# Separate rooms for results in a two-bottleneck kernel: five rooms for chunks, four for results, five for weights

## The chip, the cores and the metric

The kernel runs on one core of a Trainium2 chip, in one launch. The metric is the device time of the whole program in microseconds (us); before the change it is 2444.54 us, the median of three runs (2437.88 to 2444.91). The profiled execution, from which all other times here come, has a span of 2434.0 us.

## What is computed

The input is x with 16 images of 1024 channels and 32 x 32 pixels in float32. Two residual bottlenecks follow one another. Cut to what matters:

```python
# layer 0
h = relu(bn(conv1x1(x, w_conv1)))                 # 1024 -> 256 channels
q, k, v = relu(bn(h*wq)), relu(bn(h*wk)), bn(h*wv)  # 1x1 convolutions, 256 -> 256
att = softmax over the 3x3 neighbourhood of q . (k + pos), 32 heads of 8 channels
h = relu(bn(sum of v over the neighbourhood, weighted by att))
y = relu(bn(conv1x1(h, w_conv3)) + x)             # 256 -> 1024, residual x
# layer 1
g = relu(bn(conv1x1(y, w1)))                      # 1024 -> 256
g = relu(bn(conv3x3(g, w2)))                      # 256 -> 256
out = relu(bn(conv1x1(g, w3)) + y)                # 256 -> 1024, residual y
```

## The kernel before

An image's 1024 channels are eight chunks of 128 channels by 1024 pixels, 512 KB each. The work of the 16 images is cut into stages, whose order is written out by hand (L934 to L938): C (first 1x1 convolution, eight chunks of x), Q and V (projections to q, k and v), F (fused: third convolution of layer 0, residual x, and at once the first convolution of layer 1), W (the 3 x 3 convolution in Winograd form, four images at a time), U (last 1x1 convolution, residual y, output). Stages of different images follow each other on TensorE; a planner (`Side`, from L837) puts the attention's VectorE work and the Winograd transforms between them by estimated times. The program order on each engine is the order in which the Python code emits instructions; an engine's queue is worked off strictly in that order.

One chunk of an F or U stage goes through class `Expand` (from L367). `seed` (L375) has ScalarE (ACT) copy the residual chunk from SBUF into a PSUM tile, two chunks ahead of use. `products` (L381) lets TensorE add the eight matmul passes of the 1x1 convolution to it. `result` (L396) has ACT add the shift and apply relu, from PSUM into SBUF, and GpSimd (POOL) issues the store. In F the store goes to a DRAM room (`r`), and the SBUF result is also read by the eight passes of the next convolution (`reduce_part`, L348). In U the store goes to the output. The residual of an F stage is called s (read from x), that of a U stage r (read back from the DRAM room).

Before the change the result is written over the residual: `self.tiles[o]` keeps the tile that the seed has read, and `result` takes it again. So one of the eight rooms of the pool `xpool` serves a chunk from the start of its load to the landing of its store. The same eight rooms hold the chunks of x for the C stages and the V tiles (transformed hidden rows) of the W stages.

`more_loads` (L312) issues loads in the order of a fixed list, so long as there are credits; almost all go through POOL's queue, where the stores of results and the relays of the attention (q, k, v and position tables, L535) stand too. `free` (L334) gives a credit back. After a result it is called with `late`, which holds one credit back until the next call. The credits only set the place of a load in the queue: at run time the load waits until the room it was given is free, that is until the last reader, or the store, of its former tile is done.

Weights come in pieces of 512 KB through the SP queue (`more_weights`, L111) into `wpool`, six rooms. Four pieces are asked for at the start, and each piece done with asks for the next, so at most four are wanted at a time; pieces of w3 and u1 are loaded anew for every F stage, pieces of the others are kept if they are used again within three stages. A W stage reads 18 pieces U, each for one group of 16 matmul passes.

PSUM holds four tiles of 128 x 1024. Waits between engines and for rooms are put in by the framework.

Of the kernel before, what the change touches and what calls it, by code (L numbers as in the profile page):

```python
# [8 lines left out]
F32 = mybir.dt.float32  # L9
AF = mybir.ActivationFunctionType  # L10
# [3 lines left out]
P = 128  # L14
B, C, H, W = 16, 1024, 32, 32
HW = H * W
# [6 lines left out]
HEAD_DIM = 8  # L23
EPS = 1e-5
RELU = AF.Relu
CHUNKS = 8
NJ = 4
JROWS = H // NJ
JPIX = JROWS * W
# [7 lines left out]
NK = 4  # L37
# [9 lines left out]
PART = LINES * TR  # L47
# [24 lines left out]
def sa_bottleneck_kernel(ctx: ExitStack, tc: tile.TileContext, x, w1t, wqkvt, w3t, u1t, u2t, u3t, params, out):  # L72
    nc = tc.nc
# [1 line left out]
    ctx.enter_context(tc.manual_schedule())  # L75

    const = ctx.enter_context(tc.tile_pool(name="const", bufs=1))
    wpool = ctx.enter_context(tc.tile_pool(name="wpool", bufs=6))
    xpool = ctx.enter_context(tc.tile_pool(name="xpool", bufs=CHUNKS))
    hpool = ctx.enter_context(tc.tile_pool(name="hpool", bufs=5))  # L80
    apool = ctx.enter_context(tc.tile_pool(name="apool", bufs=1))
    ppool = ctx.enter_context(tc.tile_pool(name="ppool", bufs=2))
# [224 lines left out]
        return slice(half * HALF, (half + 1) * HALF)  # L307


    loads, loaded, stored, credits, freed = [], {}, {}, [CHUNKS], []  # L310

    def more_loads():  # L312

        while credits[0] and loads:
            kind, b, c = loads[0]
            if kind == "V":

                if forms.get((b, c[1] == 2), 0) < NK:
                    return
                src = form_room(b)[c[0], c[1]].rearrange("p k j e -> p (k j e)")  # L320
            elif kind == "r":
                if (b, c) not in stored:
                    return
                src = stored[b, c]
            else:
                src = x[b, c * P : (c + 1) * P, :]
            t = xpool.tile([P, NK * 2 * PART], F32, tag="x", name=f"{kind}_{b}_{c}".translate(str.maketrans(" ,", "__", "()")))
            t = t if kind == "V" else t[:, :HW]

            (nc.scalar if kind == "x" and b == 0 else nc.gpsimd).dma_start(t, src)  # L330
            loaded[loads.pop(0)] = t
            credits[0] -= 1

    def free(late):  # L334

        if late:
            freed.append(1)
            credits[0] += len(freed) - 1
            del freed[1:]
        else:  # L340
            credits[0] += 1 + len(freed)
            freed.clear()
        more_loads()

    def piece(name, half):
# [21 lines left out]
    class Expand:  # L367
# [2 lines left out]

        def __init__(self, name, b, kind, shift):
            self.name, self.b, self.kind, self.shift = name, b, kind, shift
            self.ahead, self.tiles = {}, {}

        def seed(self, o):  # L375
            ps = psum.tile([P, HW], F32, tag="ps", name="ps")
            t = self.tiles[o] = loaded.pop((self.kind, self.b, o))
            nc.scalar.activation(ps, t, AF.Identity)  # L378
            self.ahead[o] = ps

        def products(self, o):  # L381
            key = piece(self.name, o * 2 // NC)
# [11 lines left out]
                done_with(key)  # L394

        def result(self, o, to):  # L396
            t = self.tiles.pop(o)
            ps, to_ = self.ahead.pop(o), t

            if self.kind == "s":  # L400
                ps, to_ = ps.rearrange("p (n j) -> p j n", j=4), t.rearrange("p (j n) -> p j n", j=4)
            else:
                ps, to_ = ps.rearrange("p (j n) -> p n j", j=4), t.rearrange("p (n j) -> p n j", j=4)
            if (self.kind, self.b, o) == ("r", B - 1, NC - 1):

                one, two = slice(0, JPIX // 2), slice(JPIX // 2, JPIX)
                nc.scalar.activation(to_[:, one], ps[:, one], RELU, bias=self.shift(o), scale=1.0)
                nc.vector.tensor_scalar(to_[:, two], ps[:, two], self.shift(o), 0.0, ALU.add, ALU.max)
                nc.scalar.dma_start(to[:, :HALF], t[:, :HALF])
                nc.sync.dma_start(to[:, HALF:], t[:, HALF:])  # L410
                return t
            nc.scalar.activation(to_, ps, RELU, bias=self.shift(o), scale=1.0)  # L412
            nc.gpsimd.dma_start(to, t)  # L413
            return t
# [301 lines left out]
    def winograd_conv(b):  # L716
# [12 lines left out]
        def products(i, two):  # L729

            if i not in acc:
                acc[i] = psum.tile([P, 2, NK, NW, TILES], F32, tag="ps", name="ps")
            key = piece(f"U{i}", two)
            v = loaded.pop(("V", b, (i, two))).rearrange("p (k j e) -> p j k e", k=NK, j=2)
            for at in range(2):

                start = two == 0 or (two == 2 and at == 1)
                for n in range(NW):
                    for m in range(NW):
                        nc.tensor.matmul(  # L740
                            acc[i][:, at, :, n, :],
                            pieces[key][:, m, at, n * P : (n + 1) * P],
                            v[:, at, :, m * (TILES + TR) :][:, :, :TILES],
                            start=(start and m == 0 and n == 0),
                            stop=(m == NW - 1),
                            skip_group_check=True,
                        )
            done_with(key)
            free(False)

        def pair(t):
            return t.rearrange("p (a n t) -> p a n t", a=2, t=TILES)
# [181 lines left out]
    for text in (  # L934
# [5 lines left out]
        for word in text.split():  # L940
            b, _, of = word[1:].partition(":")
# [41 lines left out]
    def first_conv(b):  # L983

        ps = two_sums()
        for c in range(NC):
            reduce_part(c, ps, loaded.pop(("x", b, c)), "w1")
            free(False)
            if c == NC - 1:
                h = hidden[b] = hpool.tile([P, NW, HW], F32, tag="h", name=f"h_{b}")  # L990
                for n in range(NW):
                    nc.scalar.activation(  # L992
                        h[:, n, :], ps[n], RELU, bias=col("L0_conv_bn1_b", n), scale=col("L0_conv_bn1_s", n)
                    )
            yield CHUNK
# [22 lines left out]
    def fused(b, then):  # L1018

        side.finish(b)  # L1020
        if b == B - 1:
            for c in DEFERRED:
                side.first(transform(c, sources[c]) if c in sources else fetched(c), 0.0, 0.0)
        fetch_attended()
        side.until(side.ready[b])
        finish_attended(b)
        conv3 = expand("w3", b)
        conv3.src = attended.pop(b)
        following = [(conv3, o) for o in range(2, NC)] + then
        done, ps = {}, None  # L1030
        for o in range(NC + 1):
            if o < NC:
                conv3.products(o)
                room = stored[b, o] = dram.tile([P, HW], F32, tag=f"r{b}_{o}", name="r")
                done[o] = conv3.result(o, room)
                if o < len(following):
                    into, which = following[o]
                    into.seed(which)
                yield CHUNK
            if o:  # L1040
                ps = ps or two_sums()
                reduce_part(o - 1, ps, done.pop(o - 1), "u1")
                free(True)
                if o == NC:
                    side.finish_firsts()
                    for n in range(NW):
                        nc.scalar.activation(
                            hidden_rows(n), ps[n].rearrange("p (j r c) -> p j r c", j=4, c=TR), RELU,
                            bias=bn_sh[:, n : n + 1], scale=bn_inv[:, n : n + 1],
                        )  # L1050
                    if b in DEFERRED:
                        kept[b] = dram.tile([P, NW * VROWS * VW], F32, tag=f"h{b}", name="kept")
                        nc.sync.dma_start(kept[b], vh.rearrange("p r w -> p (r w)"))
                    else:
                        late = 0.0 if b % NK == NK - 1 else LATE
                        side.first(transform(b, vh), side.tensor + CHUNK + 6.0, side.tensor + late)
                yield CHUNK

    def last_sum(b, of, then):

        last = expand("u3", b)
        last.src = hidden_one[b]
        following = [(last, o) for o in of[2:]] + then
        for at, o in enumerate(of):
            last.products(o)
            if at < len(following):
                into, which = following[at]
                into.seed(which)
            last.result(o, out[b, o * P : (o + 1) * P, :])
            free(True)  # L1070
            yield CHUNK

    def seeds(at):
# [9 lines left out]
    def run(at):  # L1083
        now[0] = at
        kind, b, of = stages[at]
# [20 lines left out]
        for part in range(count):  # L1106
            if alone and then and part >= count - 2 and kind != "wino":
                into, which = then[part - count + 2]

                if which not in into.ahead and which not in into.tiles:  # L1110
                    into.seed(which)
            if made and (kind, part) in (("conv1", 4), ("u3", count - 2)):
                finish_winograd(made.pop(0))
# [76 lines left out]
```

## Time and profile before

| | |
|---|---|
| median of three runs | 2444.54 us |
| span of the profiled execution | 2434.0 us |
| TensorE matmuls (PE) busy | 2388.0 us, 98% |
| VectorE (DVE) busy | 2080.7 us, 85% |
| ScalarE (ACT) busy | 918.9 us, 38% |
| GpSimd (POOL) busy | 466.2 us, 19% |
| moved by DMA | 708.37 MB, mean 291 GB/s |
| store of a result to the output, issue to landing | 6.5 us (median) |
| load of a residual r | 5.7 us |
| load of a residual s | 6.2 us |
| load of a Winograd weight piece U | 6.8 us |

A group in the profile reads: line, engine, operation, what it writes and reads, shapes and count; then busy time and mean of one; then the time that the engine stood idle just before such instructions, and what released it. Timeline lines read: start and length in us, engine, line, operation, count, and in brackets the idle time before it and its releaser. Matmuls are pipelined and their ends are modelled, so start-to-start times say more than busy time. A float32 matmul of the program appears as two passes.

### The profile page before, as it was taken

Reading aid. Unit: us, or ns where it says so; the run is one execution under the profiler, and the core shown is the slowest. Engines: PE = TensorE matmul, PEld = TensorE weight load, DVE = VectorE, ACT = ScalarE, POOL = GpSimd, SP = SyncE. Lnnn points to the kernel's source line nnn. Section 1 sums busy time; section 2 is a strip of 40 time slices with the busy share of each in tenths; the row PEclk is TensorE's granted clock in tenths of the full one; section 3 lists DMA queues with packets and bytes.
Section 4 is the critical chain, followed back from the end, with each engine's and each line's share of the span. In section 5 each row is a group of like instructions: output and inputs, shape, how many; then the busy total and the mean of one; then the engine's idle time right before and its main releaser. Section 6 shows DMA issues by size and latency. Waiting matters only on the chain.

```text
span 2434.0 us, 18415 instructions
## 1 busy us (share of the span) xinstructions
PE 2388.0 (98%) x6144; PEld 1150.9 (47%) x6144; DVE 2080.7 (85%) x1632; ACT 918.9 (38%) x873; POOL 466.2 (19%) x854
## 2 busy tenths in 40 slices
PE   8999999999999989999999999999999999999999
PEld 3434444444475434444466434444466444444843
DVE  4899999999999999898989999799989999965700
ACT  3324142323122564443122564324222453344265
POOL 2211111111121222111111222111111221111122
PEclk9999999999999999999999999999999999999999
DMA  9968786878697899798788899688788896888888
GB/s 364 368 211 283 278 253 246 281 273 258 246 370 262 296 306 347 252 315 262 256 312 280 288 306 358 242 305 301 263 314 296 286 351 249 290 311 299 329 258 277
DMA packets 305821, 708.37 MB, mean 291 GB/s; under 512 B 20544, under 2 KB 174144, under 8 KB 297024
## 3 DMA queue, kind: packets, MB, share of 16 engines
q0 software_dynamic: 119024, 471.40, 55.0%
q1 hardware_dynamic: 185264, 231.30, 29.1%
q10 hardware_dynamic: 1440, 4.51, 0.5%
q8 instruction: 49, 0.80, 0.1%
q14 instruction: 44, 0.36, 0.0%
HBM read 432.10 MB, written 275.03 MB: 291 GB/s over the span
## 4 chain that ended last, share of the span: by engine, by line
PE 72%; DMA 11%; issue 5%; DVE 3%; POOL 2%; ACT 1%; SPq 0%; POOLq 0%; ACTq 0%; DVEq 0%
PE ps L354 32%; PE ps L385 21%; PE ps L448 11%; PE ps L740 7%; DMA out_dram<-r 7%; DMA bnk<-kp 1%; DMA U<-uw 1%; POOL r L330 1%; PE ps L486 1%; DVE acc L605 1%; DMA s<-in_x_dram 1%; DVE acc L618 1%; ACT h L992 0%; DMA pos<-by_offset 0%; POOL out_dram L413 0%
## 5 line engine op out<-in xcount | busy, mean ns | idle before, releaser
L385 PE MATMUL ps<-a,w 128*128 128x512 f32 x1024 | 460.3, 594 | 4.9 <-ACT a L644 3.0
L385 PE MATMUL ps<-y,u 128*128 128x512 f32 x1024 | 447.4, 598 | 13.8 <-ACT ps L378 13.8
L354 PE MATMUL ps<-s,u 128*128 128x512 f32 x1024 | 458.0, 592 | 2.2 <-ACT s L412 2.2
L354 PE MATMUL ps<-x,w 128*128 128x512 f32 x1024 | 443.6, 594 | 6.3 <-DMA x<-in_x_dram 6.3
L605 DVE TENSOR_TENSOR acc<-e,bnv 128x2048 f32<-128x2048 f32 x144 | 327.5, 2284 | 3.6
L554 DVE TENSOR_TENSOR prod<-qc,bnk 128x2048 f32<-128x2048 f32 x144 | 324.0, 2287 | 1.7
L385 PEld LDWEIGHTS ps<-y,u 128*128 128x128 f32 x1024 | 195.9, 192 | 263.4 <-issue 241.2
L412 ACT ACTIVATE s<-ps,par 128x1024 f32<-128x1024 f32 x128 | 142.6, 1114 | 469.0 <-PE ps L385 401.2
L385 PEld LDWEIGHTS ps<-a,w 128*128 128x128 f32 x1024 | 194.7, 191 | 252.4 <-issue 242.7
L354 PEld LDWEIGHTS ps<-x,w 128*128 128x128 f32 x1024 | 195.1, 191 | 251.5 <-issue 250.3
L354 PEld LDWEIGHTS ps<-s,u 128*128 128x128 f32 x1024 | 194.4, 190 | 247.6 <-issue 238.2
L618 DVE TENSOR_TENSOR acc<-acc 128x2048 f32<-128x2048 f32 x128 | 293.4, 2292 | 4.4
L448 PE MATMUL ps<-h,wqk 128*128 128x512 f32 x512 | 227.8, 599 | 10.5 <-ACT h L992 10.5
L413 POOL DMA_DIRECT2D r<-s x128 | 68.8, 538 | 632.7 <-ACT s L412 608.4
L412 ACT ACTIVATE r<-ps,bn_sh 128x1024 f32<-128x1024 f32 x127 | 140.5, 1107 | 83.9 <-PE ps L385 83.1
L559 DVE TENSOR_TENSOR prod<-prod 128x2048 f32<-128x2048 f32 (+1 forms) x80 | 166.2, 2077 | 2.4
L448 PEld LDWEIGHTS ps<-h,wqk 128*128 128x128 f32 x512 | 96.9, 191 | 138.9 <-issue 111.3
L378 ACT ACTIVATE ps<-r 128x1024 f32<-128x1024 f32 x128 | 130.5, 1022 | 68.9 <-DMA r<-r 61.4
L992 ACT ACTIVATE h<-ps,par 128x1024 f32<-128x1024 f32 x32 | 38.4, 1204 | 272.5 <-PE ps L354 248.1
L460 ACT ACTIVATE kp<-ps,par 128x1024 f32<-128x1024 f32 x64 | 77.4, 1210 | 167.3 <-PE ps L448 124.2
L378 ACT ACTIVATE ps<-s 128x1024 f32<-128x1024 f32 x128 | 131.2, 1025 | 22.4 <-DMA s<-in_x_dram 20.0
L330 POOL DMA_DIRECT2D r<-r x128 | 68.4, 534 | 299.4 <-DMA out_dram<-r 186.7
(317 smaller groups left out, 2288.7 us busy)
## 6 DMA issues: line engine op xcount, KB each, us to landing
s<-in_x_dram POOLq DMA_DIRECT2D x128, 512.0 KB, 6.2
r<-s POOLq DMA_DIRECT2D x128, 512.0 KB, 4.8
r<-r POOLq DMA_DIRECT2D x128, 512.0 KB, 5.7
out_dram<-r POOLq DMA_DIRECT2D x127, 512.0 KB, 6.5
x<-in_x_dram POOLq DMA_DIRECT2D x120, 512.0 KB, 5.6
v<-v SPq DMA_DIRECT2D x96, 408.0 KB, 5.6
U<-uw SPq DMA_DIRECT2D x72, 512.0 KB, 6.8
bnk<-kp SPq DMA_DIRECT2D x32, 680.0 KB, 7.4
```

The lines of the kernel that those rows point to most:

```text
L330: (nc.scalar if kind == "x" and b == 0 else nc.gpsimd).dma_start(t, src)
L354: nc.tensor.matmul(ps[n][:, halves(half)], wt[:, c % (NC // 2), n * P : (n + 1) * P], src[:, halves(half)], start=(c == 0), stop=(c == NC ...
L378: nc.scalar.activation(ps, t, AF.Identity)
L385: nc.tensor.matmul(self.ahead[o][:, halves(half)], pieces[key][:, n, o % (NC // 2) * P :][:, :P], self.src[:, n, halves(half)], start=Fals ...
L412: nc.scalar.activation(to_, ps, RELU, bias=self.shift(o), scale=1.0)
L448: nc.tensor.matmul(ps[:, halves(half)], pieces[key][:, m, at : at + P], h[:, m, halves(half)], start=(m == 0), stop=(m == NW - 1),)
L460: nc.scalar.activation(dst, src, func, bias=col(f"L0_conv_{name}_b", n), scale=col(f"L0_conv_{name}_s", n),)
L554: nc.vector.tensor_tensor(by_row(t[:, two]), by_row(qc), kc[:, :, i : i + JROWS, j : j + W], ALU.mult)
L559: nc.vector.tensor_add(u[:, :, 0:4], u[:, :, 0:4], u[:, :, 4:8])
L605: nc.vector.tensor_tensor(by_row(dst), rows(e[:, k, :]).unsqueeze(1).to_broadcast([P, HEAD_DIM, JROWS, W]), vc[:, :, i : i + JROWS, j : j ...
L618: nc.vector.tensor_add(acc, acc, t)
L740: nc.tensor.matmul(acc[i][:, at, :, n, :], pieces[key][:, m, at, n * P : (n + 1) * P], v[:, at, :, m * (TILES + TR) :][:, :, :TILES], star ...
```

## The change

The result gets a room of its own in a new pool, `rpool`, with four rooms. A residual's room in `xpool` counts as free from the moment at which the seed is emitted, and at that place `more_loads` is called. `xpool` shrinks from eight rooms to five, `wpool` from six to five, so that the SBUF needed stays about the same. The credits become a count of live chunks: at most five loads stand unread, except for the chunks of x of the first two images, when no result needs a room yet: their chunks 5 to 7 go into `rpool`, and up to eight may be live. The lagging `free(late)` is gone. The aim is that no load waits for the store of a result.

```diff
-CHUNKS = 8
+CHUNKS, RESULTS = 5, 4
...
-    wpool = ctx.enter_context(tc.tile_pool(name="wpool", bufs=6))
+    wpool = ctx.enter_context(tc.tile_pool(name="wpool", bufs=5))
     xpool = ctx.enter_context(tc.tile_pool(name="xpool", bufs=CHUNKS))
+    rpool = ctx.enter_context(tc.tile_pool(name="rpool", bufs=RESULTS))
...
-        while credits[0] and loads:
+        while loads and live[0] < CHUNKS + RESULTS - 1:
             kind, b, c = loads[0]
+
+            spare = kind == "x" and b < 2 and c >= CHUNKS
+            if live[0] >= CHUNKS and not (kind == "x" and b < 2):
+                return
...
+            if spare:
+                t = rpool.tile([P, HW], F32, tag="r", name=name)
+            else:
+                t = xpool.tile([P, NK * 2 * PART], F32, tag="x", name=name)
+                t = t if kind == "V" else t[:, :HW]
...
-            credits[0] -= 1
-
-    def free(late):
-
-        if late:
-            freed.append(1)
-            credits[0] += len(freed) - 1
-            del freed[1:]
-        else:
-            credits[0] += 1 + len(freed)
-            freed.clear()
+            live[0] += 1
+
+    def free():
+
+        live[0] -= 1
         more_loads()
...
         def seed(self, o):
             ps = psum.tile([P, HW], F32, tag="ps", name="ps")
-            t = self.tiles[o] = loaded.pop((self.kind, self.b, o))
-            nc.scalar.activation(ps, t, AF.Identity)
+            nc.scalar.activation(ps, loaded.pop((self.kind, self.b, o)), AF.Identity)
             self.ahead[o] = ps
+            live[0] -= 1
+            more_loads()
...
         def result(self, o, to):
-            t = self.tiles.pop(o)
+            t = rpool.tile([P, HW], F32, tag="r", name="result")
```

In the C and W stages `free(False)` becomes `free()`; the calls `free(True)` after a result in the F and U stages go.

More of the change, by code (lines that the diff above doesn't have):

```diff
@@ L307, in halves @@
         return slice(half * HALF, (half + 1) * HALF)
-    loads, loaded, stored, credits, freed = [], {}, {}, [CHUNKS], []
+    loads, loaded, stored, live = [], {}, {}, [0]
     def more_loads():
-        while credits[0] and loads:
+        while loads and live[0] < CHUNKS + RESULTS - 1:
             kind, b, c = loads[0]
+            spare = kind == "x" and b < 2 and c >= CHUNKS
+            if live[0] >= CHUNKS and not (kind == "x" and b < 2):
+                return
             if kind == "V":
@@ L326, in more_loads @@
                 src = x[b, c * P : (c + 1) * P, :]
-            t = xpool.tile([P, NK * 2 * PART], F32, tag="x", name=f"{kind}_{b}_{c}".translate(str.maketrans(" ,", "__", "()")))
-            t = t if kind == "V" else t[:, :HW]
+            name = f"{kind}_{b}_{c}".translate(str.maketrans(" ,", "__", "()"))
+            if spare:
[3 more added lines that the diff above has]
+                t = t if kind == "V" else t[:, :HW]
             (nc.scalar if kind == "x" and b == 0 else nc.gpsimd).dma_start(t, src)
             loaded[loads.pop(0)] = t
-            credits[0] -= 1
-    def free(late):
-        if late:
-            freed.append(1)
-            credits[0] += len(freed) - 1
-            del freed[1:]
-        else:
-            credits[0] += 1 + len(freed)
-            freed.clear()
+            live[0] += 1
+    def free():
+        live[0] -= 1
         more_loads()
@@ L372, in __init__ @@
             self.name, self.b, self.kind, self.shift = name, b, kind, shift
-            self.ahead, self.tiles = {}, {}
+            self.ahead = {}
         def seed(self, o):
             ps = psum.tile([P, HW], F32, tag="ps", name="ps")
-            t = self.tiles[o] = loaded.pop((self.kind, self.b, o))
-            nc.scalar.activation(ps, t, AF.Identity)
+            nc.scalar.activation(ps, loaded.pop((self.kind, self.b, o)), AF.Identity)
             self.ahead[o] = ps
+            live[0] -= 1
+            more_loads()
         def products(self, o):
@@ L748, in products @@
             done_with(key)
-            free(False)
+            free()
         def pair(t):
@@ L987, in first_conv @@
             reduce_part(c, ps, loaded.pop(("x", b, c)), "w1")
-            free(False)
+            free()
             if c == NC - 1:
@@ L1042, in fused @@
                 reduce_part(o - 1, ps, done.pop(o - 1), "u1")
-                free(True)
                 if o == NC:
@@ L1069, in last_sum @@
             last.result(o, out[b, o * P : (o + 1) * P, :])
-            free(True)
             yield CHUNK
@@ L1108, in run @@
                 into, which = then[part - count + 2]
-                if which not in into.ahead and which not in into.tiles:
+                if which not in into.ahead:
                     into.seed(which)
```

## The prediction, made before the result was known

> **What bounds the kernel now.** I read the page's busy line and groups first, to find the engine that is full and what it idles for; then the chain, the table of waits, and the timeline around the two longest idle times of TensorE.
>
> ```profile
> PE 2388.0 (98%) x6144; PEld 1150.9 (47%) x6144; DVE 2080.7 (85%) x1632; ACT 918.9 (38%) x873; POOL 466.2 (19%) x854
> ...
> PE ps L354 32%; PE ps L385 21%; PE ps L448 11%; PE ps L740 7%; DMA out_dram<-r 7%; DMA bnk<-kp 1%; DMA U<-uw 1%; POOL r L330 1%; PE ps L486 1%; DVE acc L605 1%; DMA s<-in_x_dram 1%; DVE acc L618 1%; ACT h L992 0%; DMA pos<-by_offset 0%; POOL out_dram L413 0%
> ...
> L385 PE MATMUL ps<-y,u 128*128 128x512 f32 x1024 | 447.4, 598 | 13.8 <-ACT ps L378 13.8
> ...
> L378 ACT ACTIVATE ps<-r 128x1024 f32<-128x1024 f32 x128 | 130.5, 1022 | 68.9 <-DMA r<-r 61.4
> ...
> L330 POOL DMA_DIRECT2D r<-r x128 | 68.4, 534 | 299.4 <-DMA out_dram<-r 186.7
> ```
>
> TensorE is full, so only its lost time can be won. In the chain, 80 matmuls in a row take 34.35 us, 0.429 each, and 288 Winograd ones 62.36, 0.2165. So 4864 x 0.429 = 2089, 1152 x 0.2165 = 249, and some 28 for the 128 position matmuls (about 0.215, two sharing the array): 2366 of the span's 2434. Of the 68 lost, 6.3 lie before the first matmul and 5 after the last. The three groups tell one story from the bottom up: POOL's load of a residual waits for an output store (187 us), ACT's seed waits for that load (61), TensorE for that seed (14). The store also holds 7% of the chain.
>
> ```profile
> POOL r L330 <- DMA out_dram<-r: 186.7, 71, 11.3
> ...
> POOL s L330 <- DMA out_dram<-r: 79.0, 25, 6.4
> ```
>
> That is 2.6 and 3.2 us a wait: the room asked for is that of the result sent one chunk (3.43 us) ago, and a store takes 6.5 (median). Before the longest (POOL alone, then all engines):
>
> ```profile
> 890.83 0.54 POOL L535 DMA_DIRECT2D qc<-q  x1
> 891.35 0.53 POOL L535 DMA_DIRECT2D bnk<-bnk  x1
> 891.88 0.53 POOL L535 DMA_DIRECT2D pc<-pos  x1
> 892.40 0.54 POOL L413 DMA_DIRECT2D out_dram<-r  x1
> 893.60 0.53 POOL L330 DMA_DIRECT2D r<-r  x1 [0.67 <-DMA out_dram<-r]
> 894.13 0.54 POOL L413 DMA_DIRECT2D out_dram<-r  x1
> ```
>
> ```profile
> 906.01 0.53 POOL L330 DMA_DIRECT2D r<-r  x1 [11.35 <-DMA out_dram<-r]
> ...
> 907.00 1.03 ACT L378 ACTIVATE ps<-r 128x1024 f32<-128x1024 f32 x1 [9.89 <-DMA r<-r]
> ...
> 908.08 8.19 PE L385 MATMUL ps<-y,u 128*128 128x512 f32 x12 [6.60 <-ACT ps L378]
> ```
>
> Three relays (2.9 MB) stand before the store of 892.40 on POOL's queue; it lands after 13.3 us instead of some 6.5. Until then POOL issues neither the next load nor the store behind it. The load of 893.60 lands at 906.9, and TensorE has stood still for 6.6. At 1455.6 the same picture returns with 5.25.
>
> ```profile
> 835.00:928.00 93.00, 85.95 (x194) 37.53 (x193) 87.69 (x51) 56.73 (x54) 23.39 (x44) 0.96 0.96 310
> ...
> 908.00:917.00 9.00, 8.92 (x15) 3.88 (x16) 8.86 (x5) 5.19 (x6) 3.18 (x6) 0.68 0.93 324
> ```
>
> The first row is the run U1 to U3: 24 chunks at 3.43 need 82.4, it takes 92.9. The second shows that the granted clock is 0.68 in the 9 us after the gap: a gap costs more than its own length.
>
> **What the Trainium skill says.** "Perfetto Trace Analysis", Optimization Strategy, holds that a gap that repeats on the saturated engine can mean too few rooms for the next tile; the trace agrees, with the refinement that eight rooms are held through the stores. "TensorE: Matmul & The Clock Gate", What's actually happening, lets the clock fall to half after about 3.4 us of idling: 0.68 above agrees, and starts after the gap lose another 2.9 us. "DMA: Bandwidth & Descriptors", SWDGE vs HWDGE vs iDMA, gives software descriptors one queue only, which all of POOL's transfers share; the 13.3 us behind the relays agree. (Its Anatomy section would price 512 KB at about 3.2 us; here it takes 4.8 to 6.5, and I use those.)
>
> **The change, part by part.**
>
> *The wait removed.* A residual's room is now free when the seed (1.02 us) has copied it, two chunks ahead of its products, and the next load is put on the queue there. POOL's order becomes load, store, load, store, each waiting for ACT alone; no load waits for a store. Five loads stand ahead of the seed, so a load has 5 x 3.43 = 17.2 us until its own seed; it needs 6 usually and 14 behind the relays. Both gaps should go. Won: at 908.1 start-to-start excess 6.8 plus 2.9 of slow matmuls; at 1455.6, 5.4 plus 2.2; and two smaller ones where the next fused stage's loads of s are late for the same reason, 2.4 at 939 and 1.8 at 1487. Sum 21.5.
>
> *Does the gain reach the end?* Later the chain runs over VectorE: at 2154 TensorE waits 2.7 us for the attended values of image 15. An earlier TensorE helps only if VectorE comes along. Between 908 and 2140 VectorE idles 10.5 us at 983, 5.6 at 1147, 8.0 at 1257, 12.9 at 1536 and 9.5 at 1810, each time for ACT's exponential or the Winograd copies, which follow TensorE. Less some 2.2 that each exponential needs anyway, 40 us can shrink; 21.5 pass. One check: at 981 the exponential would come 12 us sooner, VectorE is ready 8.4 before it, so ACT waits 3.6; behind it are the two activations of hidden rows, 2.6, and the next sums need their PSUM 6.9 after the stage: 6.2, just hidden. Cost 0, at most 3.
>
> *The wait added.* A result's ACT instruction (1.11 us) now waits until the store four results back has landed, with every later seed and result behind it, and TensorE behind the seeds. In the last-sum stages four chunks are 13.7 us; less 1.1 for the result and 0.5 for POOL the store may take 12.1. Usual 6.5: no wait. Behind relays 13.3 to 14.1: ACT waits 1 to 2 us. A seed is due two chunks (6.9 us) after the result before it, result plus seed take 2.1, so 4.7 us of delay are free. In fused stages a chunk is 6.9 us, four are 27. Cost 0, at most 4.
>
> *Fewer rooms for chunks, 8 to 5.* In the convolution stages POOL issues a load 0.3 us after the chunk whose room it takes; five rooms leave 13.7 us, and in the stages concerned these loads land in 3.7 to 10.4. Winograd tiles last 3.46 us each, leaving 13.8; they land in 4.3 to 11.8 in the first three Winograd stages and in up to 14.7 in the fourth, where four to five in flight push one another. With fewer in flight they should be quicker. At the very first images the extra rooms keep eight in flight. Cost 0, at most 3.
>
> *Weights, 6 rooms to 5.* Only four pieces are wanted at once, so one room is still spare. In a Winograd stage a piece is loaded when the one six before it is done, then when the one five before is: 13.8 us ahead instead of 17.3, against landings of 3.2 to 16. The longest (14 to 16, first stage) are those queued with eight V tiles; five tiles relieve them. The last Winograd stage keeps two pieces of u3, so four rooms turn and then three: 6.9 us ahead. Landings there are 4 to 8.4, about 7 in the middle. At 6.9 nothing is lost; at 7.6 a piece takes (7.6 + 3.46) / 3 = 3.69, and 14 pieces lose 3.2; at 8.4 they lose 6.9. Since results no longer hold the tiles' rooms there, the 1.6 us gap at 2250.9 may go. Low -1.6, high 7; I take +1.
>
> *Nothing:* bytes, matmuls and activations are the same; the SBUF taken is nearly the same (a partition: 6 x 4 + 8 x 4.25 = 58 KB before, 5 x 4 + 5 x 4.25 + 4 x 4 = 57 after).
>
> Sum: 21.5 - 1 = 20.5 off. From the median, 2444.5 - 20.5 = **2424**.
>
> **The rivals.** *(1) Transfers take it back.* The run U1 to U3 moved 310 GB/s with the engines busy 0.96; without the gap the same 28.8 MB need 356. Against it: after the relays 512 KB land every 1.2 us, some 430 GB/s. For it: small packets from SP run beside these. If half of each gap stays, 10 are won: 2434. *(2) The wait only moves.* ACT stands for the store as POOL did, at both relays and where many transfers run at once, and the last Winograd stage pays 3 to 5: nothing is won, 2441 to 2447. For it speaks that ACT's order is strict and four rooms exceed a usual store by 2 only; against it the 4.7 us of slack. *(3) Slower.* Shorter leads bite in the Winograd and convolution stages: three Winograd stages and the convolutions lose some 5 each, the last Winograd stage 7, 27 in all against 15 won: 2456. Against it: the three first stages show landings under 13.8 but for three pieces of weights.
>
> **How the numbers follow.** My forecast 0.62, (1) 0.14, (2) 0.11, (3) 0.13. More than 0.3% is 7.3 us: faster takes the forecast and two thirds of (1), 0.71; the same takes the rest of (1) and most of (2), 0.15; slower 0.14. Range: below, 21.5 plus the 1.6 and a spread of the runs of some 7 give 2414; above, it includes (1) and half of (2), 2442.
>
> **What would show it.** Right: in the waits, POOL's loads r and s no longer wait for output stores but for ACT's seeds; the gaps at 908 and 1456 vanish and U1 to U3 take under 85 us; ACT's wait for r<-r falls well below 61; VectorE's idle times at 983 and 1536 shrink. A line ACT r L412 waiting for out_dram appears, under 15 us in all. Wrong: that line with some 50 us and TensorE waiting for seeds again; TensorE waiting for DMA U or V in the last Winograd stage for over 5 us; a longer wait for image 15's attended values, which would mean that VectorE did not come along.

## The result, and the profile after

The changed kernel takes **2423.99 us**, the median of four runs (2422.09 to 2425.53). The kernel before, run beside it, takes 2442.58 (four runs, 2437.88 to 2444.91). The ratio is 0.9926 with a 95% interval of 0.9907 to 0.9945: 18.6 us, 0.74% less. In a later set of runs the same kernel gave 2422.58 (six runs) and 0.9942 [0.9922, 0.9963], some 14 us less than before.

The profiled executions differ by less, in their spans by 10.3 us (2434.0 to 2423.7): the one of after was the slowest of its four runs, 1.5 us over their median, and the one of before, at 2435.75 us of device time, was 6.8 under the median of 2442.58. So the profiles show where the time goes, and the runs how much it is; where the slower runs of before spend those 6.8 us no trace shows.

The page of the kernel after: the busy line, the chain, and the groups that told the story before.

```profile
PE 2386.1 (98%) x6144; PEld 1151.4 (48%) x6144; DVE 2080.9 (86%) x1632; ACT 917.9 (38%) x873; POOL 467.8 (19%) x854
...
PE ps L389 25%; PE ps L357 24%; PE ps L744 9%; PE ps L452 6%; DVE acc L609 4%; DVE prod L558 4%; DVE acc L622 4%; DVE prod L563 2%; DMA uw<-u 2%; DMA U<-uw 2%; DMA v<-v 1%; DVE form L673 1%; DVE prod L564 1%; DVE v L673 1%; POOL out_dram L417 1%
...
L389 PE MATMUL ps<-y,u 128*128 128x512 f32 x1024 | 443.2, 594 | 3.0 <-ACT ps L380 3.0
...
L380 ACT ACTIVATE ps<-r 128x1024 f32<-128x1024 f32 x128 | 130.6, 1021 | 27.6 <-DMA r<-r 20.1
```

The store, which held 7% of the chain, is gone from the entries shown, and VectorE's attention sums have come in (`acc`, `prod`). TensorE's wait for the seeds of U stages fell from 13.8 us to 3.0, the seeds' wait for the residual from 61.4 to 20.1. In the table of waits the seed has taken the store's place as what POOL's loads wait for:

```profile
POOL r L339 <- ACT ps L380: 108.9, 91, 9.5
ACT e L590 <- DVE e L587: 85.5, 12, 24.5
POOL s L339 <- ACT ps L380: 76.6, 97, 6.4
...
ACT result L416 <- DMA out_dram<-result: 7.8, 7, 3.0
```

Loads of r no longer wait for an output store at all, loads of s once, for 0.4 us. The last line is the wait that the change adds: 7.8 us in all, and no TensorE gap follows from it. The longest of its seven waits can be seen in the timeline behind the relays of U3, where TensorE runs through:

```profile
894.78 20.76 PE L389 MATMUL ps<-y,u 128*128 128x512 f32 x48
...
901.94 0.54 POOL L417 DMA_DIRECT2D out_dram<-result  x1 [1.71 <-DMA pc<-pos]
...
904.00 1.12 ACT L416 ACTIVATE result<-ps,bn_sh 128x1024 f32<-128x1024 f32 x1 [3.04 <-DMA out_dram<-result]
...
905.01 1.02 ACT L380 ACTIVATE ps<-r 128x1024 f32<-128x1024 f32 x1
```

ACT stands 3.04 us for a result's room, the next seed comes that much later, and the 48 passes go on in one row of 20.76 us.

Stage by stage, from TensorE's first pass to its last, in us; the last column is how much later (+) or earlier the stage ends after the change than before, in the two profiles:

| stage | before | after | end shifted by |
|---|---|---|---|
| F3 | 55.1 | 55.7 | about +1.3 |
| W0 | 63.6 | 66.7 | +4.4 |
| U1 to U3 | 92.9 | 86.5 | -2.0 |
| F4 to F7 | 222.4 | 219.9 | -4.6 |
| U5 to U7 | 90.2 | 82.6 | -12.2 |
| F8, F9 | 111.9 | 110.0 | -14.0 |
| F15 (starts 1.7 later by its own wait) | 57.5 | 59.3 | -10.4 |
| W12 | 64.0 | 65.5 | -8.9 |
| last run of U | 122.6 | 121.6 | -9.9 |

So 6.4 + 2.5 + 7.6 + 1.8 + 1.0 = 19.3 us were won in U1 to F7, U5 to F9 and the last run of U, and some 9.4 given back in W0, F15, W12 and before them, in this pair of executions.

### The profile page after: what moved, and what is told of

Its sections match the earlier page's. It is cut to its first block, busy times and chain, and to the rows that moved or that the text cites. A ratio compares the mean times of both kernels' runs of the same rounds, so it can differ in the third digit from the quotient of the medians.

```text
span 2423.7 us, 18498 instructions
## 1 busy us (share of the span) xinstructions
PE 2386.1 (98%) x6144; PEld 1151.4 (48%) x6144; DVE 2080.9 (86%) x1632; ACT 917.9 (38%) x873; POOL 467.8 (19%) x854
## 4 chain that ended last, share of the span: by engine, by line
PE 64%; DVE 23%; DMA 6%; issue 4%; POOL 1%; ACT 1%; POOLq 0%; SPq 0%; ACTq 0%; DVEq 0%
PE ps L389 25%; PE ps L357 24%; PE ps L744 9%; PE ps L452 6%; DVE acc L609 4%; DVE prod L558 4%; DVE acc L622 4%; DVE prod L563 2%; DMA uw<-u 2%; DMA U<-uw 2%; DMA v<-v 1%; DVE form L673 1%; DVE prod L564 1%; DVE v L673 1%; POOL out_dram L417 1%
## 5 line engine op out<-in xcount | busy, mean ns | idle before, releaser
L357 PE MATMUL ps<-result,u 128*128 128x512 f32 x1024 | 457.8, 592 | 0.3 <-ACT result L416 0.3
L357 PEld LDWEIGHTS ps<-result,u 128*128 128x128 f32 x1024 | 194.4, 190 | 245.6 <-issue 237.0
L416 ACT ACTIVATE result<-ps,par 128x1024 f32<-128x1024 f32 x128 | 142.6, 1114 | 442.7 <-PE ps L389 379.4
L452 PE MATMUL ps<-h,wqk 128*128 128x512 f32 x512 | 227.4, 598 | 12.2 <-ACT h L996 12.2
L416 ACT ACTIVATE result<-ps,bn_sh 128x1024 f32<-128x1024 f32 x127 | 141.4, 1113 | 133.6 <-PE ps L389 125.5
L417 POOL DMA_DIRECT2D r<-result x128 | 69.0, 539 | 631.4 <-ACT result L416 616.5
L380 ACT ACTIVATE ps<-r 128x1024 f32<-128x1024 f32 x128 | 130.6, 1021 | 27.6 <-DMA r<-r 20.1
L339 POOL DMA_DIRECT2D x<-in_x_dram x120 | 64.0, 534 | 289.4 <-PE ps L357 224.7
```

Source lines behind the costliest of these rows:

```text
L357: nc.tensor.matmul(ps[n][:, halves(half)], wt[:, c % (NC // 2), n * P : (n + 1) * P], src[:, halves(half)], start=(c == 0), stop=(c == NC ...
L380: nc.scalar.activation(ps, loaded.pop((self.kind, self.b, o)), AF.Identity)
L452: nc.tensor.matmul(ps[:, halves(half)], pieces[key][:, m, at : at + P], h[:, m, halves(half)], start=(m == 0), stop=(m == NW - 1),)
```

## The experiments

The kernels e1, e2 and e4 are edits of the kernel before, the others of the kernel after. All ratios are to the kernel before on the same chip, whose medians there were 2437.5 to 2438.9 us.

**One weight room less, alone.**

```diff
-    wpool = ctx.enter_context(tc.tile_pool(name="wpool", bufs=6))
+    wpool = ctx.enter_context(tc.tile_pool(name="wpool", bufs=5))
```

> The kernel before with five rooms for weights instead of six and nothing else. My theory: this part alone costs, in the Winograd stages only: in the first (W0) up to 3 us, because pieces are asked for one piece later while many transfers run, in the last (W12) 1 to 2 us, where three rooms turn instead of four; 2 to 5 us in all, the two long gaps in U1 to U3 and U5 to U7 stay. Rival: a spare room for weights is worth nothing, 0 within 2 us, and the time lost in W0 and W12 comes from the fewer rooms for chunks.

Measured: 2441.89 us, 1.0013 [1.0005, 1.0021], some 3 slower. W0 took 70.4 and W12 67.3 (before: 63.6 and 64.0), but this profiled execution was 7.4 us above the median of its runs, and W0's part has a cause of its own, shown below under weights. U1 to U3 and U5 to U7 still took 92.0 and 90.7. The price of a weight room is small but clear of noise, and none of the gain comes from it.

**Nine rooms for both, still shared.** Chunks and results keep one pool, which gets all nine rooms of the change:

```diff
-CHUNKS = 8
+CHUNKS = 9
...
-    wpool = ctx.enter_context(tc.tile_pool(name="wpool", bufs=6))
+    wpool = ctx.enter_context(tc.tile_pool(name="wpool", bufs=5))
```

> The kernel before with nine shared rooms for chunks and results (as many as five plus four) and five for weights: the same SBUF as the change, but results still lie over their residuals. My theory: the load still waits for a store, so POOL's waits for output stores stay near 187 and 79 us; one more room only gives 3.4 us more lead, which shortens each long gap by about 3.4 us and some slow matmuls; U1 to U3 take some 87 us, 6 to 10 us are won in all before what the weights cost. Rival: what helps is the number of rooms; then the gaps vanish as in the change and 15 to 20 us are won.

Measured: 2440.01 us, 1.0001 [0.9989, 1.0014]. The waits of this kernel:

```profile
POOL r L330 <- DMA out_dram<-r: 185.2, 68, 12.1
...
POOL s L330 <- DMA out_dram<-r: 88.1, 29, 7.6
...
ACT ps L378 <- DMA r<-r: 26.3, 10, 7.3
```

The ninth room gives the loads a longer lead (the seeds' wait falls from 61 to 26 us, the U runs to 87.6 and 88.2, F4 to F7 to 220.1: 9.7 us in these three), but POOL stands for the stores as long as before, 185 and 88 us, F8 and F9 lose 2.1, and the Winograd stages lose 9 in this execution. In the runs the kernel is no faster than before; against e1, which has the same five weight rooms, it gains some 3 us (1.0001 against 1.0013), which the intervals don't tell from nothing, where I had expected 6 to 10. So one more shared room hides a part of the wait and doesn't end it; with the same rooms divided, so that no load depends on a store, the gain is there. Ten shared rooms or more were not tried. "Perfetto Trace Analysis", Optimization Strategy, on which the prediction leaned, says that a repeated gap can mean too few rooms; here one more room, in the same pool, bought nothing clear of noise.

**The relays on another queue.** In the kernel before, the attention's relays go to SP's queue, so that no 2.9 MB stand before a store on POOL's:

```diff
-            nc.gpsimd.dma_start(t.rearrange("p d w -> p (d w)"), backs[name])
+            nc.sync.dma_start(t.rearrange("p d w -> p (d w)"), backs[name])
```

> The kernel before with the relays of the attention (q, k, v and position tables) issued from SP's queue instead of POOL's; the stores no longer stand behind them. My theory: the long gaps start with the relays, so stores in U1 to U3 and U5 to U7 land in 6 to 9 us, both runs take some 84 to 86 us instead of 92.9 and 90.2, and 8 to 15 us are won unless weights now stand behind the relays on SP; POOL's many short waits for output stores stay. Rival: the short waits alone are the cause (a store's 6.5 us for every two chunks), the gaps stay at 5 us or more.

Measured: 2447.29 us, 1.0035 [1.0022, 1.0047]. A verdict in two parts. SP works its queue in order as well, and a relay that waits there holds up what is behind it. At the first attention SP issued nothing from 80.5 us until the relay `bnv<-bnv` at 93.6; the stores `uw<-u` behind it went out from 94.0, ACT had waited 11.9 us for them and TensorE 13.9 for ACT, and the kernel lost 9.8 there. In U1 to U3 and U5 to U7 the gaps of 6.6 and 5.25 us are gone, and none is over 2 us. But both runs are longer than expected, 90.8 and 87.7 us instead of 84 to 86: POOL's loads of r and s still wait 162 and 95 us for stores, and TensorE's waits for seeds come to 12.8 us in 19 short gaps (before: 15.6 in 7). Gaps in F8 cost 5 more. So the relays make the two gaps long, and the room held through the store keeps the many short waits.

**Three rooms for results.** The first try also lowered the limit of chunks waiting in the first two images from eight to seven:

```diff
-CHUNKS, RESULTS = 5, 4
+CHUNKS, RESULTS = 5, 3
```

> The changed kernel with three rooms for results instead of four. My theory: a store may now take 3 x 3.43 - 1.6 = 8.7 us before ACT stands; usual ones take 6.1, so only the stores behind the relays (13) make ACT wait, some 4 to 5 us each time, and TensorE, which has 4.7 us of slack, loses 0 to 2 us each: 0 to 5 us slower than the change, ACT's wait for stores at 15 to 40 us instead of 7.8. Rival A: four rooms were already the limit, ACT waits at nearly every chunk, over 15 us slower. Rival B: nothing changes at all, ACT's wait stays below 10.

Measured: 2441.39 us, 1.0018 [1.0008, 1.0027], 17 slower than the change where at most 5 were expected. Five of it were lost in the first images, with a gap of 10.3 us at 95.6, for which the lower limit is the suspect. So it was run again with the limit kept:

```diff
-CHUNKS, RESULTS = 5, 4
+CHUNKS, RESULTS = 5, 3
...
-        while loads and live[0] < CHUNKS + RESULTS - 1:
+        while loads and live[0] < 8:
```

> The changed kernel with three rooms for results, as in the run before, but with eight chunks allowed in flight for the first two images, which that run had cut to seven. My theory after that run: the 5 us lost before the first fused stage were the seventh chunk and go; what the missing result room costs stays: U5 to U7 some 7 us and the fused stage after it some 5, U1 to U3 1, so 8 to 13 us slower than the change. Rival: the loss in U5 to U7 was a matter of where the relays fell in that run; then it is within 4 us of the change.

Measured: 2436.95 us, 0.9992 [0.9983, 1.0001]: 13 slower than the change, nearly the whole gain gone. Its waits, and its timeline behind the relays of U7:

```profile
ACT result L416 <- DMA out_dram<-result: 41.7, 15, 8.8
```

```profile
1440.70 1.11 ACT L416 ACTIVATE result<-ps,bn_sh 128x1024 f32<-128x1024 f32 x1 [6.80 <-DMA out_dram<-result]
...
1443.98 1.01 ACT L380 ACTIVATE ps<-r 128x1024 f32<-128x1024 f32 x1
...
1445.04 7.18 PE L389 MATMUL ps<-y,u 128*128 128x512 f32 x11 [5.16 <-ACT ps L380]
```

This is the rival "the wait only moves", made visible. With three rooms ACT waits 6.8 us for a store, the seed behind it is late, and TensorE stands 5.16, the length of the gap of before. The slack of 4.7 us that I gave ACT holds a wait of 3.04 with four rooms, and not one of 6.80 with three, the less so as ACT had 2.36 us of hidden rows to do before the seed. In U3 of this kernel, without such work in between, a wait of 5.41 us left a gap of 0.81.

**Other sizes of the three pools.** Four chunks, four results, six weights; then four, five, five. Both keep the limit of eight at the start, as in the last diff:

```diff
-CHUNKS, RESULTS = 5, 4
+CHUNKS, RESULTS = 4, 4
...
-    wpool = ctx.enter_context(tc.tile_pool(name="wpool", bufs=5))
+    wpool = ctx.enter_context(tc.tile_pool(name="wpool", bufs=6))
```

> The changed kernel with four rooms for chunks, four for results and six for weights (eight chunks in flight for the first two images). My theory: the weights' share of the loss in W0 and W12 comes back (W0 from 66.7 towards 64, W12 from 65.5 towards 64), and the chunks' lead of 3 x 3.43 = 10.3 us in convolutions and Winograd stages and 13.7 in last sums is a little too short behind the relays and at the start of W0: 0 to 6 us slower than the change in all. Rival: chunk rooms are plenty; 3 to 5 us faster than the change.

```diff
-CHUNKS, RESULTS = 5, 4
+CHUNKS, RESULTS = 4, 5
```

> Four rooms for chunks, five for results, five for weights, eight early chunks. Theory: three rooms for results lost 12 us and four make ACT wait 8 us for stores in all, none of it long enough to stop TensorE; a fifth is worth 0 to 2 us. Rival: the curve goes on, 4 to 8 us faster than the change.

Measured: 2424.81 us, 0.9946 [0.9930, 0.9961], and 2425.94, 0.9955 [0.9939, 0.9972], neither to be told from the change. In e12 ACT never waits for a store any more, and nothing is won by it. Three, four and five rooms for results give 2437, 2423 and 2426 (the last with a chunk room less): four are enough. In e6 the sixth weight room did not make W12 shorter (69.4 us, against 65.5 with five).

**The load asked for later.** The room is separate as in the change, but the next load is put on POOL's queue behind the result's store instead of at the seed, some 3 us later:

```diff
             live[0] -= 1
-            more_loads()
...
             nc.gpsimd.dma_start(to, t)
+            more_loads()
             return t
```

> The changed kernel with the next load asked for after a result's store is put on the queue, not at the seed; it still waits for no store. My theory: what counts is that the load does not wait for the store's landing; the load comes 1 to 2 us later, five chunks of lead hide it, 0 to 3 us slower than the change, U1 to U3 and U5 to U7 stay under 88 and 84 us. Rival: the earlier place in POOL's queue is what brought the gain; then more than 8 us slower.

Measured: 2424.32 us, 0.9943 [0.9927, 0.9960], the same as the change; U1 to U3 84.6, U5 to U7 82.6. So the place in the queue is not what pays. The free room is.

**The wait put back, with rooms of their own.** To e7 a write of POOL is added: ahead of the next load it overwrites one column of the result sent before, and so it must wait for that store to land; the column has been sent by then.

```diff
             nc.gpsimd.dma_start(to, t)
+            if self.kind == "r":
+                if sent:
+                    nc.gpsimd.memset(sent.pop()[:, 0:1], 0.0)
+                sent.append(t)
             more_loads()
...
-    sums = {}
+    sums, sent = {}, []
```

> The changed kernel with the load asked for after the store (as in the run before that did this, 2424.3) and with the old wait put back alone: in the last sums POOL writes one column of the result before (a tiny memset, no output changes), which must wait until that result's store has landed, and only then issues the next load. Rooms stay five, four and five. My theory: this wait is what the change removed; POOL waits some 150 us for output stores again, gaps return behind the relays, and 8 to 18 us are lost. Rival: separate rooms and the missing lag in the count brought the gain; 0 to 3 us lost.

Measured: 2465.89 us, 1.0115 [1.0097, 1.0133], 41.6 slower than e7. The waits:

```profile
POOL result L419 <- DMA out_dram<-result: 284.0, 109, 10.4
...
ACT ps L380 <- DMA r<-r: 66.8, 38, 9.6
...
ACT result L415 <- POOL result L419: 60.7, 47, 8.6
...
PE ps L388 <- ACT ps L380: 18.6, 12, 5.4
```

The direction is as expected, and the pattern of before is back: POOL for the store, ACT for the load, TensorE for the seed (67 and 19 us; in the same table before 61 and 16). U1 to U3 took 92.0 us and U5 to U7 91.5, against 92.9 and 90.2 before. The size is two to five times what I expected: the delay also reached the fused stages (F4 to F7 228.3 us, before 222.4), for which the five rooms for chunks are the likely reason, and ACT's results wait 60.7 us for POOL's write, which has no counterpart before. So the experiment shows what a wait for a store does at this place, and its 41.6 us are no measure of the wait that the change removed.

**One more piece of weights asked for ahead**, as five rooms allow:

```diff
         hooks["conv1", 2, 0] = clear_hidden
+        hooks["conv1", 3, 0] = more_weights
```

> The changed kernel with one more piece of weights asked for from the fourth image on (five instead of four), so that SP meets a load of weights one piece earlier in its queue and the fourth U piece of W0 no longer stands behind the store of k. My theory: that piece comes some 3 us sooner and W0 takes about 64 us instead of 66.7, W12 stays at 65.5: 2 to 3 us faster than the change. Rival: SP now stands before a full room with the stores of k behind it, or the transfers set the pace; no gain, up to 5 us slower.

Measured: 2427.22 us, 0.9956 [0.9940, 0.9972]. W0 64.4, as expected, W12 67.0 and F15 65.0: no gain, and the longer lead of the weights did not shorten W12.

**The change once more**, beside these:

> The changed kernel itself, beside the three others and more runs of the kernel before. Theory: 12 to 18 us faster than before, and in a second profile the fused stages and both runs of last sums take the same time within 1 us as in the first, while W0, which took 62.7 to 70.4 us in the profiles so far without following the number of rooms, may differ by some us.

Measured: the 2422.58 us given above. Its second profile has W0 at 70.2, U5 to U7 at 82.6 and W12 at 65.1: the gain in the U runs repeats to 0.1 us in U5 to U7 (U1 to U3: 87.0), while W0 moves by 3.5 between two executions of one kernel, and F15 by 2.3 (57.1), where I had expected no more than 1.

**Four chunks, six weights and the late request together** (the edits of e6 and e7):

> A candidate: four rooms for chunks, four for results, six for weights, eight early chunks, and the load asked for after the store. Theory: every one of these was worth 0 to 2 us alone, so the time is that of the change within 3 us. Rival: with only four chunks ahead the later request is seen; 4 to 8 us slower.

Measured: 2442.09 us, 1.0019 [1.0012, 1.0027], 17 slower than either alone; I had expected no more than 3. The waits of this kernel:

```profile
ACT ps L380 <- DMA r<-r: 58.8, 20, 10.1
...
PE ps L388 <- ACT ps L380: 11.0, 6, 6.8
...
PE ps L744 <- DMA U<-uw: 6.1, 1, 6.1
```

The seeds wait for loads again, with one TensorE gap of 6.8 us in U1 to U3, which takes 91.6 us (e6 84.0, e7 84.6). That is some 7 of the 17; U5 to U7 lose 2 to 3 more, and the rest lies for the most part in F15 and W12, which vary from run to run. Counted from the row of chunks: five rooms give a load 17.2 us, four 13.7; asking 3 us later leaves 14.2 of five and 10.7 of four, and behind the relays a load needs up to 14. Each step by itself just fits, the two don't. The counting is argued from the landing times; that the two steps fit singly and cost 17 us together is shown.

## Why the prediction was right

**The wait removed.** Right, in mechanism and sum. I predicted 21.5 us at four places; the stages show 6.4 in U1 to U3, 7.6 in U5 to U7, 2.5 in F4 to F7 and 1.8 in F8 and F9, 18.3 together. The 1.0 in the last U run is not the separate rooms' doing: e1 and e2 have it too. Both gaps, at 908 and 1456, are gone. e2 and e4 separate the parts of the cause, the shared room and the relays, and e10 brings the pattern back. U1 to U3, which I put under 85, took 86.5, because a gap at their start, of 0.45 us before the change, grew to 1.94:

```profile
846.60 1.21 ACT L464 ACTIVATE kp<-ps,par 128x1024 f32<-128x1024 f32 x1 [7.89 <-DMA bnk<-kp]
...
848.78 7.54 PE L389 MATMUL ps<-y,u 128*128 128x512 f32 x13 [1.94 <-ACT ps L380]
```

ACT waits 7.89 us for the room of a key table whose store is late (6.41 before), and the seed behind it in ACT's order comes late by 1.94. The repeat (e9) has 2.51 at this place, and e1 and e2, whose rooms are shared, have 2.84 and 2.00, so the separate rooms don't make it; what delays the store stays open. In e7 it is 0.36, and U1 to U3 take 84.6.

**Does the gain reach the end?** Right in the main. VectorE came along: its idle times at 983, 1147, 1257, 1536 and 1810 fell from 10.5, 5.6, 8.0, 12.9 and 9.5 us to 2.2, 2.1, 7.1, 3.4 and 5.6, and ACT's exponential waits for VectorE 85.5 us in all instead of 65.3. The shift of -14.0 at F9 still stood at TensorE's last pass ahead of F15 (it ends at 2151.54 before the change, 2137.55 after). The sign that I had named for a failure, a longer wait for image 15's attended values, did come, though not through VectorE: its last sum of image 15 was done 14.0 us sooner, but the loads that turn the values round landed less soon.

```profile
2133.55 1.10 SPq L640 DMA_DIRECT2D a<-a  x2
...
2140.63 1.25 ACT L648 ACTIVATE a<-a,par 128x1024 f32<-128x1024 f32 x1 [1.93 <-DMA a<-a]
...
2141.93 1.29 PE L389 MATMUL ps<-a,w 128*128 128x512 f32 x2 [4.38 <-ACT a L648]
...
2143.05 1.24 ACT L648 ACTIVATE a<-a,par 128x1024 f32<-128x1024 f32 x1 [1.17 <-DMA a<-a]
...
2144.34 8.01 PE L389 MATMUL ps<-a,w 128*128 128x512 f32 x12 [1.13 <-ACT a L648]
```

The first was issued 13.4 us earlier than before (2146.96 there), and ACT could read them 12.3 and 11.3 us earlier. With the longer start this cost 3.5 us, a term that I had at nothing. The cost is no constant: 1.2 us in e9, 8.5 in e7. Loads of s, which the change lets run further ahead, move beside them; that these are the cause is argued, not shown, and in e1 and e4, whose rooms are shared, the second of these loads took 8.9 and 9.9 us as well (7.0 before, 9.1 after).

**The wait added.** Right: 7.8 us of waiting in all, no gap behind it, and e12 wins nothing by removing it. Behind the two relays ACT waited 3.0 and 2.4 us, a little over the 1 to 2 reckoned. How far the margin reaches, e5 shows: a room less, and 13 us are lost.

**Fewer rooms for chunks.** Right at nothing: e6 and e12 do with four.

**Weights.** The term that was mis-sized. I took +1 (range -1.6 to 7); in the profile W0 pays 3.2 and W12 1.5, 4.7 in all, and e1 pays 3.2 in its runs. That a piece is asked for when the one five before is done, and in W12 the one three before, could be seen in the issue times as reckoned. The landings that follow from it could not: the fifth piece of W0 took 16.1 us, and I had expected five V tiles to relieve it. But W0 varies: with five weight rooms it took 62.7, 62.8, 66.7 and 70.2 us in e7, e12, the change and e9. Most of this is not the weights. In the longest cases another store holds a room, as in e9:

```profile
705.93 1.02 ACT L767 ACTIVATE z<-ps 128x1024 f32<-128x1024 f32 x1 [9.20 <-DMA pos<-by_offset]
...
707.01 2.50 PE L744 MATMUL ps<-V__2_2386,U 128*128 128x256 f32 x5 [4.43 <-ACT z L767]
```

ACT's copy of the Winograd sums (`z`) takes its rooms from the same pool of three as the position table, whose store has to land first, and TensorE stands until the copy frees its sums. ACT waited 8.9 to 9.2 us for it in e1, e2 and e9 (W0 68.8 to 70.4), and in e7 and e12, where the store landed in time, the plain 2.5 for TensorE's sums. In the change the same copy waited 5.9, and then the late piece of weights held TensorE, 2.06 us in all. Why that store lands early or late stays **open**. W12 is not ordered by the weight rooms either (six: 64.0 before, 69.4 in e6; five: 64.4 in e5 to 67.9 in e12). In W12 TensorE waited for weights twice, 2.7 us together, under the 5 named as a bad sign:

```profile
2240.32 3.69 PE L744 MATMUL ps<-V__1_8219,U 128*128 128x256 f32 x16 [1.24 <-DMA U<-uw]
...
2252.39 3.69 PE L744 MATMUL ps<-V__2_8281,U 128*128 128x256 f32 x16 [1.48 <-DMA U<-uw]
```

**The rivals.** "Transfers take it back" fell in the U runs. Without the gaps they moved more, as these windows of the kernel after show (the last three columns are the granted clock, the share of the DMA engines and GB/s):

```profile
839.80:926.30 86.50, 84.56 (x194) 37.17 (x193) 78.36 (x47) 57.14 (x55) 26.72 (x50) 0.98 1.00 371
1387.30:1469.80 82.50, 82.50 (x194) 36.58 (x193) 78.94 (x48) 57.52 (x55) 27.22 (x51) 1.00 0.99 378
```

With the engines busy all the time 371 to 378 GB/s were to be had, more than needed: the prediction's 28.8 MB in 82.4 us are 350 GB/s, not 356. At F15 it may hold a little, which is not shown. "The wait only moves" holds for three rooms, not for four. "Slower" needed shorter leads to bite, which they do only when two of them come together (e11).

The sum: 18.6 us by the runs, some 14 in the later set, against 20.5 predicted. That the median fell on the predicted 2424 to the microsecond is luck: the kernel before came out 2 us lower beside it (2442.58, not 2444.54), and that made up for the 2 us by which the gain fell short. In the profile the places won less than reckoned (18.3 of 21.5), and W0, F15 and W12 gave back more than the 1 us allowed for.

## What to carry to other kernels

A buffer that is read in and sent out again binds the load to the store, and on an in-order queue one late store then holds up everything behind it; give the outgoing data a pool of its own before adding rooms to the shared one, and look for other pools of this kind (here the position table and the Winograd copies). Then count the rooms of the new pool from the longest landing of a store, not the usual one, since the wait is now on the engine that writes the results (here four rooms hide it and three lose nearly all the gain). And when two edits each shorten a lead and each costs nothing, cost them together: e6 and e7 were free, their sum lost 17 us.

## What the runs showed of the hardware

A short gap is not always free of the clock. After the gap of 1.94 us at 848.8 the granted clock was 0.81 in the next 9.0 us, a further 9.0 x 0.19 = 1.7 us, nearly the gap's own length again; after the 6.6 us gap of before it was 0.68. But after the gap of 2.25 us at 939.2 of before it stayed at 1.00. In the fourteen profiles, from 60 us on, all 47 gaps over 3.0 us were followed by a stretch at half clock, 13 of 23 between 1.9 and 3.0 us, and 4 of 234 between 0.4 and 1.9 us, each of these just behind a longer gap. "TensorE: Matmul & The Clock Gate", What's actually happening, gives an idle window of about 3.4 us for the fall; here less was enough in some cases, and the measurement decides.

Loads and stores of chunks of 512 KB through POOL's queue took 4.8 to 6.9 us in the median (of each kind, before and after) and 13.3 to 14.1 behind the relays in U3 before the change. In the trace of before none of POOL's 845 transfers was issued before the one eight places ahead of it had landed, so at most eight were in flight at a time.
